# Three matmul passes of split FP32 operands in one PSUM bank instead of two, with another third form of the tokens

## The chip, the cores and the metric

The kernel runs on one NeuronCore of a Trainium2 chip. A core has a matmul engine (TensorE, PE in the profile; its weight loads are PEld), VectorE (DVE), ScalarE (ACT), GpSimd (POOL) and SyncE (SP), which run their own instruction streams and wait for each other on semaphores. Matmuls write to PSUM, which the kernel uses as eight banks of 512 FP32 values in each of 128 partitions. The metric is the device time of one execution in microseconds (us). Lower is better.

## What is computed

Input `x` is (32, 64, 1024) in FP32, with one conditioning row of 128 for each of the 32 samples. Two layers follow one another, each with a residual. The reference, cut to what matters here:

```python
def _L0_ffn_ref(x, A, B, Wr):              # A: (64, 16, 1024), B: (64, 1024, 16)
    scores = xf @ Wr.T                     # 64 experts
    top_vals, top_idx = jax.lax.top_k(scores, 16)
    gates = jax.nn.softmax(top_vals, axis=-1)
    G = zeros.at[rows, top_idx].set(gates)
    h = jnp.einsum('nd,krd->nkr', xf, A)
    out = jnp.einsum('nkr,kdr->nd', h * G[:, :, None], B)
    return out * 2.0

x = x + _L0_ffn_ref(_cond_ref(x, cond_512, ...), A, B, Wr)
x = x + _L1_ffn_ref(_cond_ref(x, cond_512, ...), qweight, scales, zeros, bias)
```

`_cond_ref` is a chain of four modulated convolutions of 3 taps over the 1024 positions (same, upsample, same, downsample), with weights that depend on the sample. `_L1_ffn_ref` is a dense product with a 1024 x 1024 matrix whose entries are unpacked from 4-bit integers.

## The kernel before

**Pairs.** Two samples of 64 channels fill the 128 partitions, so there are 16 pairs in each layer. A pair's convolution result, turned so that the 1024 positions lie on the partitions in 8 blocks of 128, is called its tokens.

**Three phases.** First, for each pair of layer 0: convolutions (`first`, `rest`), then `layer0`, the product with `wa`, which is the router and A side by side (1024 x 1088), then the gates (top 16 of 64, softmax) and their multiplication into the result (`gated`, line 1003, on GpSimd). The result goes to DRAM. Second, for each pair: load it again, transpose it on TensorE (`turned_h`), and in `layer0b` multiply by B (`wb`, 1024 x 1024) and add the residual. Third, for each pair of layer 1: convolutions, and `layer1`, the product with the unpacked matrix. Around 0 to 100 us the layer's factors are made; around 400 to 437 `wb` is prepared; from 590 to 660 the second phase overlaps with the first convolutions of layer 1.

**Split operands.** In this trace a 128x512 matmul on the type fp32r takes TensorE 0.23 us, while one on plain FP32 is two instructions of 0.43 us. So operands are split into an upper part, with its last 12 bits cleared, and the rest, and multiplied as fp32r in several passes. `split` (line 915) makes the upper part of the tokens, `th`, by a shift on VectorE (`high`, line 149) and a copy on ScalarE (line 923), and the lower part, `tl`, on VectorE (line 919). `split_weights` (line 367) does so with the weights, into three forms per block of 128 rows: 0 the upper part (ScalarE, line 375), 1 the lower part (GpSimd, line 374), and 2 the crossed form, upper minus R times lower (VectorE, line 382), with R = 2**12. The first two pairs of layer 0 (`WHOLE`) use plain FP32 instead, while the weights are being split.

**Three passes.** Before the change, `tl` is multiplied by R on ScalarE right after its split (`scaled_low`, line 927). A third form, `td` = `th` - R `tl`, is made by `crossed` on GpSimd (line 935) at the end of the previous pair's turn; it has one buffer. With these, `product` runs passes 0 and 1 (called `Q`: `th` with the upper weights, R `tl` with the lower ones) into one PSUM bank, and pass 2 (called `D`: `td` with the crossed weights) into another. The exact product is (1 + 1/R) times the first bank minus 1/R times the second. `joined` forms it: in `layer0` the first bank by ScalarE (line 976) and then the second by VectorE (line 977); in `layer0b` two VectorE instructions, the second bank into the residual (line 1123) and the first bank plus the residual (line 1124).

**Chunks.** `layer0` cuts the 1088 columns in three (352, 368, 368): Q of chunks 0 and 1, then D of both, then Q and D of chunk 2. Pair 2, the first with split operands, does blocks 0 to 5 of every pass first and then blocks 6 and 7, whose weights are split late. `layer0b` has two chunks of 512: Q, Q, D, D. The last pair goes block by block.

**PSUM.** Three pools share the eight banks: `cps` has three (convolutions, line 832's first reconstruction result, transposes), `mps` one and `fps` four (the products). The second reconstruction result (line 872) lies in `cps`, except in layer 1 from its second pair on, where it lies in `fps`. It is freed by line 919.

**Order.** The order of instructions on each engine is fixed before the run by a planner that goes by the order of the program, by its own estimate of when operands are ready and by free buffers. So program order is followed loosely: matmuls of a convolution stand between those of a product. At run time every engine works strictly in that order.

**Weights of the second phase.** Blocks 0 to 3 of `wb` are split during pair 0 of `layer0b`, blocks 4 to 7 during pair 1; pair 2 is the first to use them.

Of the kernel before, what the change touches and what calls it, by code (L numbers as in the profile page):

```python
# [11 lines left out]
AF = mybir.ActivationFunctionType  # L12
ALU = mybir.AluOpType
# [12 lines left out]
H = 512  # L26
# [6 lines left out]
SCALING = 2.0  # L33
# [7 lines left out]
RADIX = float(1 << BITS)  # L41
# [22 lines left out]
def adaln_ffn_kernel(ctx: ExitStack, tc: tile.TileContext, t, out: bass.AP):  # L64
    nc = tc.nc
# [19 lines left out]
    def fpst(name):  # L85
        return fps.tile([P, H], F32, tag="fps", name=name)
# [67 lines left out]
    done, tbl, outers, uppers = {}, {}, {}, {}  # L154
    WHOLE = (0, 1)
# [624 lines left out]
    def rest(i, n, y, f):  # L780
# [4 lines left out]
        p, h = n // 2, n % 2  # L785
        whole = i == 0 and p in WHOLE
        key = f"x{i}_{p}"
        if h == 0:
            th = tokens("th", f"th{key}", F32 if whole else F32R)
            toks[key] = [th] if whole else [th, tokens("tl", f"tl{key}")]  # L790
        hs = halves[h]
        th = toks[key][0][:, :, hs]
# [7 lines left out]
        if whole:  # L800
            yb, yo = y
            ps = cpst(f"r{i}_{n}")
            for j in range(4):
                for k in range(4):
                    v = (yo, yb)[(j + k) % 2]
                    o = j // 2 + k // 2 + (j % 2) * (k % 2)
# [4 lines left out]
                        start=(k == 0),  # L811
                        stop=(k == 3),
                    )
            c = tbl[i, p][:, h, 1].unsqueeze(1).to_broadcast([P, 2 * 4, C])
# [17 lines left out]
        ps = cpst(f"r{i}_{n}_0")  # L832
        for j in range(2):
# [4 lines left out]
                start=True,  # L838
                stop=True,
            )  # L840
        for j in range(2):
            if nine(i, p):
# [4 lines left out]
                    start=True,  # L847
                    stop=True,
                )
                continue  # L850
            for k in range(2):
# [4 lines left out]
                    start=(k == 0),  # L856
                    stop=(k == 1),
# [11 lines left out]
            m.rearrange("p (q b) -> p q b", q=2).unsqueeze(1).to_broadcast([P, 2, 2, P]),  # L869
            ALU.add,  # L870
        )
        ps = (fpst if i == 1 and p > 0 else cpst)(f"r{i}_{n}_1")
        for j in range(4):
            q, k = j % 2, j // 2
            done["r"] = nc.tensor.matmul(  # L875
# [3 lines left out]
                start=True,  # L879
                stop=True,  # L880
# [6 lines left out]
            re[:, p % 2, h].unsqueeze(1).to_broadcast([P, 2, P]),  # L887
        )
        split(ps, shape, th, toks[key][1][:, :, hs], f"h{i}_{p}_{h}", i == 1 and h == 1 and p > 0)
        if i == 0 and h == 1:  # L890
            scaled_low(toks[key][1])

    def outer(p):

# [27 lines left out]
        else:  # L922
            nc.scalar.copy(hi, h)

    def scaled_low(v):
        v = v.rearrange("p a b -> p (a b)")
        nc.scalar.activation(v, v, AF.Copy, scale=RADIX)  # L927

    toks = {}

    def crossed(key):

        if key in toks and len(toks[key]) == 2:
            td = tokens("td", f"td{key}")
            done["td"] = nc.gpsimd.tensor_tensor(  # L935
                *(v.rearrange("p a b -> p (a b)") for v in (td, *toks[key])), ALU.subtract
            )
            toks[key].append(td)

    def at(k):  # L940
# [3 lines left out]
    def product(chunk, key, ws, order, limbs, ks=range(NC), first=0, last=NC - 1):  # L944


        banks, cols = chunk
        n = len(toks[key])
        for l in limbs:
            if l < n:  # L950
                for k in ks:
                    w = ws[k]
                    if n > 1:
                        w = w[:, l]
                    nc.tensor.matmul(  # L955
                        banks[l == 2],
                        toks[key][l][:, order(k)],
                        w[:, cols],
                        start=(k == first and l != 1),
                        stop=(k == last and l in (2, min(n, 2) - 1)),  # L960
                    )

    Q, D = (0, 1), (2,)
# [1 line left out]
    def layer0(p, ws):  # L965

        hs = wk.tile([P, AW], F32, tag="w4", name=f"hs{p}", bufs=3)
        key = f"x0_{p}"
        whole = p in WHOLE

        def joined(col, w, qd):
            dst = hs[:, col : col + w]
            if whole:
                nc.scalar.copy(dst, qd[0])
                return
            nc.scalar.activation(dst, qd[0], AF.Copy, scale=1.0 + 1.0 / RADIX)
            nc.vector.scalar_tensor_tensor(dst, qd[1], -1.0 / RADIX, dst, ALU.mult, ALU.add)

        ga = tiny.tile([P, E], F32, tag="ga", name=f"ga_{p}")

# [24 lines left out]
        def chunk(c):  # L1005
            a, b = CHUNKS[c]
            w = (b - a) * R + (E if c == 0 else 0)
            col = a * R + (E if c > 0 else 0)
            banks = [fpst(f"h{p}_{c}_{j}")[:, :w] for j in range(1 if whole else 2)]
            return banks, slice(col, col + w)  # L1010

        def done_with(c, ch):
            product(ch, key, ws, at, D)
# [56 lines left out]
    def turned_h(p, hg):  # L1070
        whole = p in WHOLE
        key = f"h{p}"
        th = tokens("th", f"th{key}", F32 if whole else F32R)
        toks[key] = [th] if whole else [th, tokens("tl", f"tl{key}")]
        for g in range(2):
            ps = cpst(f"ht{p}_{g}")
            for c in range(4):
                k = 4 * g + c
                nc.tensor.transpose(  # L1079
                    ps[:, c * P : (c + 1) * P], hg[:, k * P : (k + 1) * P], ident  # L1080
                )
            ks = slice(4 * g, 4 * g + 4)

            def d(v):
                return v[:, ks].rearrange("p a b -> p (a b)")

            if whole:
                nc.scalar.copy(d(th), ps)
            else:
                split(ps, lambda v: v, d(th), d(toks[key][1]), f"hh{p}_{g}")  # L1090
        if not whole:
            scaled_low(toks[key][1])

    residual = {}

# [11 lines left out]

    def layer0b(p, ws):

        whole = p in WHOLE  # L1110
        key = f"h{p}"
        xres = residual.pop(p)
        x1 = wk.tile([P, L], F32, tag="w4", name=f"x1_{p}", bufs=3)
        x4 = x1.rearrange("p (f j) -> p j f", f=4)

        def banks(c):
            return [fpst(f"o{p}_{c}_{j}") for j in range(1 if whole else 2)]

        def joined(c, qd):
            cs = slice(c * H, (c + 1) * H)  # L1120
            v = xres[:, cs]
            if not whole:
                nc.vector.scalar_tensor_tensor(v, qd[1], -SCALING / RADIX, v, ALU.mult, ALU.add)  # L1123
            nc.vector.scalar_tensor_tensor(  # L1124
                x4[:, c * P : (c + 1) * P],
                qd[0].rearrange("p (j f) -> p j f", f=4),
                SCALING if whole else SCALING * (1.0 + 1.0 / RADIX),
                v.rearrange("p (j f) -> p j f", f=4),
                ALU.mult,
                ALU.add,  # L1130
            )

        cols = [slice(c * H, (c + 1) * H) for c in range(2)]
        if p == NP - 1:
            qds = [banks(c) for c in range(2)]

            for part in (Q, D):
                for k in range(4):
                    for ch in zip(qds, cols):
                        product(ch, key, ws, lambda k: k, part, (k,))  # L1140
            yield
            for ch in zip(qds, cols):
                product(ch, key, ws, lambda k: k, Q, range(4, NC))
                yield
            for c, ch in enumerate(zip(qds, cols)):
                product(ch, key, ws, lambda k: k, D, range(4, NC))
                joined(c, qds[c])
                if c == 0:
                    yield
        else:  # L1150
            qds = [banks(c) for c in range(2)]
            for ch in zip(qds, cols):
                product(ch, key, ws, lambda k: k, Q)
            for c, ch in enumerate(zip(qds, cols)):
                product(ch, key, ws, lambda k: k, D)
                joined(c, qds[c])
                yield
        if p not in WHOLE:
            load_residual(p + 1)
# [384 lines left out]
```

## Time and profile before

| | us |
|---|---|
| median of 3 runs | 894.1 |
| the runs | 894.0, 894.1, 895.79 |
| span of the profiled execution, first to last instruction | 893.1 |
| TensorE busy | 866.1 |
| VectorE busy | 723.2 |
| ScalarE busy | 352.4 |
| GpSimd busy | 531.1 |

The profile gives the span of the execution that it shows, not a time of its own; the median of the runs lies 1.0 us above that span. "Busy" is time in which an instruction of the engine runs; matmuls overlap, and their ends are modelled. In a timeline, a line holds the start, the duration, the engine, the line of the kernel, the operation, the output and the input, their shapes and the number of instructions merged; in brackets stand the idle time before them and who ended it. Busy time of the groups of instructions that the change touches, with the mean of one:

| line, engine | what | count | us | mean ns |
|---|---|---|---|---|
| 976, ACT | first bank of a chunk of `layer0` | 42 | 19.9 | 473 |
| 977, DVE | second bank of it | 42 | 22.0 | 525 |
| 1123, DVE | second bank into the residual, `layer0b` | 28 | 18.0 + 1.4 | 692 |
| 1124, DVE | first bank plus residual | 26 + 6 | 28.4 + 6.1 | 1091, 1076 |
| 927, ACT | `tl` times R | 14 + 14 | 14.8 + 14.8 | 1056, 1060 |
| 935, POOL | `td` | 14 + 14 | 34.7 + 34.0 | 2479, 2425 |
| 382, DVE | crossed weights, `wa` and `wb` | 8 + 8 | 11.8 + 15.8 | 1472, 1975 |

### The profile page before, as it was taken

To read this page: it belongs to the slowest core of one execution; us is meant where nothing else is said; L and a number is where in the kernel's file an instruction comes from. 1 tells how busy PE (TensorE), PEld (TensorE's weight loads), DVE (VectorE), ACT (ScalarE), POOL (GpSimd) and SP (SyncE) were. 2 spreads that over 40 slices of the span, in tenths; PEclk is the share of its full clock that TensorE was granted. 3 is DMA by queue.
4 is the path that set the end of the run, shared out by engine and by line. 5 is a ranking of instruction groups with operands and counts; after the bars stand their busy time and mean duration, and the time that the engine had idled before them with its cause. 6 is when DMAs were issued, how large, how long until landed. Compare 5 with 4: busy or idle time off the path is not lost.

```text
span 893.1 us, 14916 instructions
## 1 busy us (share of the span) xinstructions
PE 866.1 (97%) x5033; PEld 775.1 (87%) x5033; DVE 723.2 (81%) x1460; ACT 352.4 (39%) x817; POOL 531.1 (59%) x745
## 2 busy tenths in 40 slices
PE   6989999999999999999999999999999999999997
PEld 4876888999999999994688888888899999999997
DVE  4475898888888888778986765669999999999996
ACT  6444544444444444333332221247333433343340
POOL 7235654666666666556572222343787888888884
PEclk9999999999999999999999999999999999999999
DMA  8632222222232222345475666555543334334321
GB/s 240 155 73 54 54 69 62 88 89 80 79 91 83 81 79 71 106 178 149 139 232 193 201 193 197 189 192 167 164 117 111 98 100 143 114 90 139 122 66 71
DMA packets 49739, 109.81 MB, mean 123 GB/s; under 512 B 13700, under 2 KB 22400, under 8 KB 49664
## 3 DMA queue, kind: packets, MB, share of 16 engines
q1 hardware_dynamic: 48704, 107.88, 39.5%
q10 hardware_dynamic: 960, 0.99, 0.5%
q8 instruction: 40, 0.66, 0.3%
q14 instruction: 35, 0.29, 0.1%
HBM read 70.97 MB, written 37.88 MB: 122 GB/s over the span
## 4 chain that ended last, share of the span: by engine, by line
PE 42%; DVE 7%; POOL 2%; issue 2%; ACT 0%; DVEq 0%; POOLq 0%; ACTq 0%
PE o L955 16%; PE q L1204 11%; PE f L619 3%; PE r L875 3%; PE c L773 2%; PE r L834 1%; PE r L843 1%; PE c L768 1%; PE ht L1079 1%; PE g L596 1%; DVE cv L716 1%; DVE x L1124 1%; PE p L826 1%; DVE rt L866 1%; DVE r L884 0%
## 5 line engine op out<-in xcount | busy, mean ns | idle before, releaser
L716 DVE TENSOR_TENSOR cv<-cv 128x257 f32<-128x257 f32 x120 | 105.8, 913 | 1.3 <-ACT cv L758 0.9
L730 POOL TENSOR_TENSOR cv<-cv 128x256 f32<-128x256 f32 x120 | 77.7, 647 | 29.8 <-DVE cv L716 25.1
L722 POOL TENSOR_TENSOR cv<-cv 128x128 f32<-128x128 f32 x100 | 39.0, 411 | 67.5 <-PE r L843 48.3
L1204 PE MATMUL q<-wq,thx 128*128 128x342 f32 x384 | 73.0, 332 | 2.1 <-ACT thx L913 2.1
L955 PE MATMUL h<-wa,tdx 128*128 128x352 f32 (+1 forms) x336 | 72.2, 351 | 0.2 <-DVE wa L382 0.2
L1204 PE MATMUL q<-wq,tlx 128*128 128x342 f32 x384 | 72.3, 330 | 0.0
L619 PE MATMUL f<-gs,iw 128*128 128x128 f32 (+1 forms) x384 | 68.2, 327 | 0.1
L619 PEld LDWEIGHTS f<-gs,iw 128*128 128x128 f32 x384 | 61.8, 190 | 5.9 <-issue 0.5
L955 PE MATMUL h<-wa,thx 128*128 128x352 f32 (+1 forms) x336 | 64.7, 333 | 0.0
L1204 PEld LDWEIGHTS q<-wq,thx 128*128 128x128 f32 x384 | 60.3, 189 | 4.1 <-ACT thx L913 3.2
L770 ACT ACTIVATE yt<-c,be,al 128x257 f32<-128x257 f32 x56 | 31.7, 567 | 80.4 <-PE c L768 77.3
L875 PE MATMUL r<-cv 128*128 128x128 f32 x480 | 63.4, 274 | 0.0
L1204 PEld LDWEIGHTS q<-wq,tlx 128*128 128x128 f32 x384 | 61.9, 189 | 0.8
L955 PE MATMUL h<-wa,tlx 128*128 128x352 f32 (+1 forms) x336 | 62.4, 327 | 0.0
L955 PE MATMUL o<-wb,thh 128*128 128x512 f32 x224 | 60.4, 402 | 1.5 <-ACT wb L375 1.5
L935 POOL TENSOR_TENSOR tdx<-thx,tlx 128x1024 fp32r<-128x1024 f32 x14 | 34.7, 2479 | 44.5 <-ACT tlx L927 36.2
L955 PEld LDWEIGHTS h<-wa,tdx 128*128 128x128 f32 x336 | 56.9, 188 | 2.4 <-DVE wa L382 0.5
L1123 DVE SCALAR_TENSOR_TENSOR cv<-o,cv 128x512 f32<-128x512 f32 x26 | 18.0, 692 | 50.2 <-PE o L955 50.2
L955 PE MATMUL o<-wb,tlh 128*128 128x512 f32 x224 | 58.4, 397 | 0.0
L875 PEld LDWEIGHTS r<-cv 128*128 128x128 f32 x480 | 58.4, 191 | 0.0
L634 ACT COPY cv<-f 128x256 f32<-128x256 f32 x64 | 24.0, 375 | 83.9 <-PE f L619 46.3
L642 POOL TENSOR_TENSOR cv<-cv 128x256 f32<-128x256 f32 x60 | 50.0, 833 | 11.4 <-ACT cv L637 11.4
(313 smaller groups left out, 2274.6 us busy)
## 6 DMA issues: line engine op xcount, KB each, us to landing
cv<-in_x_dram SPq DMA_DIRECT2D x60, 256.0 KB
cv<-x1e SPq DMA_DIRECT2D x64, 192.5 KB
x1e<-dd SPq DMA_DIRECT2D x16, 514.0 KB
hgd<-hs SPq DMA_DIRECT2D x16, 512.0 KB
hg<-hgd SPq DMA_DIRECT2D x16, 512.0 KB
x1d<-x SPq DMA_DIRECT2D x16, 512.0 KB
xb<-x1d SPq DMA_DIRECT2D x16, 512.0 KB
out_dram<-o SPq DMA_DIRECT2D x15, 512.0 KB
```

The lines of the kernel that those rows point to most:

```text
L619: done["f"] = nc.tensor.matmul(pv[:, n : n + 2 - k], iw[:, e].rearrange("p a b -> p (a b)"), v, start=(m == 0), stop=(m == len(steps) - 1) ...
L634: nc.scalar.copy(f8[:, 0::2], pv[:, :, h])
L642: nc.gpsimd.tensor_tensor(f[:, 4 * P : 6 * P].rearrange("p (a b) -> p a b", b=P), v[:, :, 0], v[:, :, 1], ALU.add,)
L716: nc.vector.tensor_tensor(d[:, k], yo[:, k : k + HQ], yb, ALU.subtract)
L722: nc.gpsimd.tensor_tensor(y[:, YB + k * P : YB + (k + 1) * P], y[:, 2 * k : 2 * k + 2 * P - 1 : 2], y[:, 1 : 2 * P : 2], ALU.subtract,)
L730: nc.gpsimd.tensor_tensor(e[:, :, k], d[:, :, 2 * k : 2 * k + HQ - 2 : 2], d[:, :, 1 : HQ - 1 : 2], ALU.subtract,)
L770: nc.scalar.activation(yt, mid, AF.Identity, bias=be0[:, n : n + 1], scale=a)
L875: done["r"] = nc.tensor.matmul(ps[:, j * P : (j + 1) * P], y[:, YE + (2 * q + k) * P : YE + (2 * q + k + 1) * P], w(q + 2 * k), start=True ...
L935: done["td"] = nc.gpsimd.tensor_tensor(*(v.rearrange("p a b -> p (a b)") for v in (td, *toks[key])), ALU.subtract)
L955: nc.tensor.matmul(banks[l == 2], toks[key][l][:, order(k)], w[:, cols], start=(k == first and l != 1), stop=(k == last and l in (2, min(n ...
L1123: nc.vector.scalar_tensor_tensor(v, qd[1], -SCALING / RADIX, v, ALU.mult, ALU.add)
L1204: nc.tensor.matmul(ps, half[:, k], wq[at(k)][:, c * QC : (c + 1) * QC], start=(k == 0 and j == 0), stop=(k == NC - 1 and j == 1),)
```

## The change

The algebra of the three passes is another. With `th`, `tl` the parts of the tokens and wh, wl those of the weights:

- before: bank one = th wh + (R tl) wl, bank two = (th - R tl)(wh - R wl), product = (1 + 1/R) one - 1/R two
- after: one bank = th wh + tl (wh - R wl) + ((R + 1) tl + th) wl, which is the product itself

So `tl` is no longer scaled, `td` is (R + 1) `tl` + `th`, made by a ScalarE activation into `td` and a GpSimd addition in place, the second pass uses the crossed weights (form 2) and the third the lower ones (form 1). All three passes accumulate in one bank, a chunk takes one bank of `fps`, and the joins shrink: a ScalarE copy in `layer0`, one VectorE instruction in `layer0b`. The second reconstruction result always lies in `fps`. The order of the calls is the same.

```diff
@@ rest
-        ps = (fpst if i == 1 and p > 0 else cpst)(f"r{i}_{n}_1")
+        ps = fpst(f"r{i}_{n}_1")
...
         split(ps, shape, th, toks[key][1][:, :, hs], f"h{i}_{p}_{h}", i == 1 and h == 1 and p > 0)
-        if i == 0 and h == 1:
-            scaled_low(toks[key][1])
@@ crossed
             td = tokens("td", f"td{key}")
-            done["td"] = nc.gpsimd.tensor_tensor(
-                *(v.rearrange("p a b -> p (a b)") for v in (td, *toks[key])), ALU.subtract
-            )
+            v, th, tl = (v.rearrange("p a b -> p (a b)") for v in (td, *toks[key]))
+            nc.scalar.activation(v, tl, AF.Copy, scale=RADIX + 1.0)
+            done["td"] = nc.gpsimd.tensor_tensor(v, v, th, ALU.add)
@@ product
-        banks, cols = chunk
-        n = len(toks[key])
+        bank, cols = chunk
+        n = 3 if len(toks[key]) > 1 else 1
...
-                        w = w[:, l]
+                        w = w[:, (0, 2, 1)[l]]
                     nc.tensor.matmul(
-                        banks[l == 2],
+                        bank,
                         toks[key][l][:, order(k)],
                         w[:, cols],
-                        start=(k == first and l != 1),
-                        stop=(k == last and l in (2, min(n, 2) - 1)),
+                        start=(k == first and l == 0),
+                        stop=(k == last and l == n - 1),
                     )
@@ layer0
-        def joined(col, w, qd):
+        def joined(col, w, bank):
             dst = hs[:, col : col + w]
-            if whole:
-                nc.scalar.copy(dst, qd[0])
-                return
-            nc.scalar.activation(dst, qd[0], AF.Copy, scale=1.0 + 1.0 / RADIX)
-            nc.vector.scalar_tensor_tensor(dst, qd[1], -1.0 / RADIX, dst, ALU.mult, ALU.add)
+            nc.scalar.copy(dst, bank)
...
-            banks = [fpst(f"h{p}_{c}_{j}")[:, :w] for j in range(1 if whole else 2)]
-            return banks, slice(col, col + w)
+            return fpst(f"h{p}_{c}")[:, :w], slice(col, col + w)
@@ turned_h
-        if not whole:
-            scaled_low(toks[key][1])
@@ layer0b
-        def joined(c, qd):
-            cs = slice(c * H, (c + 1) * H)
-            v = xres[:, cs]
-            if not whole:
-                nc.vector.scalar_tensor_tensor(v, qd[1], -SCALING / RADIX, v, ALU.mult, ALU.add)
+        def joined(c, bank):
             nc.vector.scalar_tensor_tensor(
                 x4[:, c * P : (c + 1) * P],
-                qd[0].rearrange("p (j f) -> p j f", f=4),
-                SCALING if whole else SCALING * (1.0 + 1.0 / RADIX),
-                v.rearrange("p (j f) -> p j f", f=4),
+                bank.rearrange("p (j f) -> p j f", f=4),
+                SCALING,
+                xres[:, c * H : (c + 1) * H].rearrange("p (j f) -> p j f", f=4),
                 ALU.mult,
                 ALU.add,
             )
```

## The prediction, made before the changed kernel was run

> **What bounds the kernel now.** I read the page's busy times first, then the busy time of each engine in six stretches, then what TensorE waited for, then the timeline around the places where it waited.
>
> The page, parts 1 and 2:
>
> ```profile
> PE 866.1 (97%) x5033; PEld 775.1 (87%) x5033; DVE 723.2 (81%) x1460; ACT 352.4 (39%) x817; POOL 531.1 (59%) x745
> ...
> PE   6989999999999999999999999999999999999997
> ```
>
> TensorE is idle for 893.1 - 866.1 = 27.0 us in all. The change alters no count and no shape of matmul (three passes before, three after), so this is all it can win. By stretch (columns: span, then PE, PEld, DVE, ACT, POOL busy, granted clock, DMA share, GB/s):
>
> ```profile
> 60.00:160.00 100.00, 96.08 (x538) 82.32 (x538) 71.24 (x163) 43.05 (x95) 53.44 (x63) 1.00 0.25 69
> 160.00:360.00 200.00, 200.00 (x1251) 190.43 (x1251) 173.60 (x409) 92.49 (x212) 120.75 (x165) 1.00 0.26 78
> 360.00:435.00 75.00, 73.46 (x354) 55.86 (x353) 57.63 (x98) 26.65 (x61) 46.76 (x51) 0.99 0.46 147
> 435.00:600.00 165.00, 164.16 (x800) 137.03 (x799) 111.71 (x183) 46.59 (x95) 55.42 (x92) 1.00 0.60 194
> 600.00:720.00 120.00, 116.50 (x743) 108.23 (x742) 115.85 (x232) 50.60 (x123) 87.23 (x138) 1.00 0.44 135
> 720.00:860.00 140.00, 140.00 (x919) 134.96 (x918) 134.14 (x253) 56.82 (x147) 118.55 (x156) 1.00 0.38 116
> ```
>
> From 160 to 360 (layer 0, first products) and from 435 to 600 (second products) TensorE has no gap worth naming. VectorE works 87% and 68% of the time there, beside it, so taking work from it buys nothing. Only 60:160, the change of phase near 430, and 600:720, where VectorE is 97% busy, leave TensorE something to win. The first 60 us (11.4 us idle) and the last 33 (5.8) hold nothing that the change touches. The waits of TensorE (total, times, longest):
>
> ```profile
> PE c L773 <- DVE rt L866: 2.2, 3, 1.1
> PE q L1204 <- ACT thx L913: 2.1, 3, 0.9
> PE r L834 <- POOL cv L648: 1.9, 2, 1.1
> PE c L773 <- DVE tlx L919: 1.8, 2, 1.3
> PE o L955 <- ACT wb L375: 1.5, 2, 0.9
> ```
>
> **Part by part.** *The joins* (edits in `layer0` and `layer0b`). Gone from VectorE: 42 of line 977 at 525 ns (22.0 us) and 28 of line 1123 (18.0 + 1.4 us), 41.4 us in all. On ScalarE the 42 of line 976 (473 ns) become copies; line 974, the same copy of a whole pair, takes 454. They now stand after the third pass. No DMA is added; the stores of lines 1063 and 1160 follow their joins and come up to 0.7 us earlier. The path that sets the end gets nothing from this wherever TensorE is full.
>
> *The third form.* Line 927 (ScalarE, 28 times 1.06 us) goes, an activation of the same size comes, and GpSimd's addition of 2.4 to 2.5 us stays. But the activation writes `td`, which has one buffer, so ScalarE now waits for the last matmul of the pair before, where GpSimd waited. Behind it stand the copies of the composed filters (lines 634 to 637) and `yt` (line 770), which sums and matmuls wait for. In the steady part of layer 0, GpSimd ran so:
>
> ```profile
> 282.29 2.50 POOL L935 TENSOR_TENSOR tdx<-thx,tlx 128x1024 fp32r<-128x1024 f32 x1 [3.59 <-ACT tlx L927]
> ...
> 287.62 0.45 POOL L652 TENSOR_TENSOR cv<-cv 128x128 f32<-128x128 f32 x1
> ```
>
> Line 927 ran at 281.16, the last third-pass matmul ended at 281.19: both conditions are met at the same moment, so nothing moves, except that ScalarE also has the 0.47 us copy of the third chunk there. Line 652 ends at 288.07 and TensorE's line 826, which needs it, starts at 288.20: a margin of 0.13 us. I take 0, since the gating at line 1003 (0.99) can use the time while ScalarE works. The bounds: 0 below (there is no TensorE gap to win) and 0.47 - 0.13 = 0.34 us in each of 13 pairs, 4.4, above. Without line 927, ScalarE's 0.16 us waits before it end too, but the upper half's pass hides them.
>
> *The banks.* The second reconstruction result moves to the pool of four, and a chunk takes one bank, not two. The waits at line 773 for lines 866 and 919 are waits for a bank of the pool of three: 1.12 us at 113.07, 0.57 at 125.00, 1.26 at 620.32.
>
> *The start of the three passes* (pair 2, 103 to 136). The 1.12 us is won, then lost: VectorE is busy without a gap from 109.9, and the crossed weights of block 7 (line 382, 118.11 + 1.29 = 119.40), now needed by the second pass, hold TensorE there. Behind the release stand three matmuls where it was one: +0.3. The 0.57 goes: -0.6. Then GpSimd's `td`, at 127.16 straight after the last matmul of pair 2, comes 1.06 + 0.1 later, and its chain to line 834 (waited for 1.15 us at 135.34) with it: +1.1, less the 0.3 by which that matmul is earlier and 0.3 for three joins less on VectorE. Sum +0.5. Bounds: -0.9 (the 1.15 goes as well, less 0.3 for the release) and +1.2 (the whole move of the chain).
>
> *The crossed weights of the second matrix* (pair 2 of `layer0b`) carry the largest term. TensorE, then VectorE:
>
> ```profile
> 432.28 0.50 PE L955 MATMUL o<-wb,thh 128*128 128x512 f32 x1 [0.91 <-ACT wb L375]
> 432.62 3.37 PE L955 MATMUL o<-wb,tlh 128*128 128x512 f32 x8
> 435.78 2.24 PE L955 MATMUL o<-wb,thh 128*128 128x512 f32 x8
> ```
>
> ```profile
> 433.00 2.31 DVE L382 SCALAR_TENSOR_TENSOR wb<-wb 128x1024 fp32r<-128x1024 f32 x1
> 436.48 1.23 DVE L382 SCALAR_TENSOR_TENSOR wb<-wb 128x1024 fp32r<-128x1024 f32 x1 [1.18 <-POOL wb L374]
> ```
>
> The second pass begins at 432.62 and used the lower weights, which were there. Now it needs the crossed ones, of which block 6 is ready at 435.31 and block 7 at 437.71. Eight matmuls took 3.37, 0.42 each: six end at 435.1, the seventh at 435.7, the eighth starts at 437.7 and ends at 437.95. The other chunk's first pass then starts at 437.95, not 435.78: +2.2. Everything on TensorE stands behind that eighth matmul: its order is fixed before the run. No cover is left, since 435:600 is full. I expect that order unchanged: VectorE ran line 382 of block 7 and even line 212 (437.62) ahead of pair 1's second join (438.49), which shows that the planner thought the weights ready before pair 1's matmuls ended.
>
> A gap also costs clock. Granted clock (column after POOL) behind the two gaps of 0.63 and 0.91 us:
>
> ```profile
> 433.00:434.00 1.00, 1.00 (x4) 0.80 (x3) 1.00 (x2) 0.89 (x4) 1.00 (x1) 0.50 0.94 352
> ...
> 436.00:437.00 1.00, 1.00 (x5) 0.78 (x5) 0.52 (x1) 0.93 (x3) 0.88 (x9) 0.85 0.00 0
> ```
>
> It stood at half for about 3.4 us (432.9 to 436.3), which is 1.7 us of work. A new gap of 2.0 us I price the same: +1.7. About 0.1 comes back, because the other chunk's first pass leaves the old slow stretch. Sum +3.8; bounds 0 (no wait) and 2.2 + 2 x 1.7 = 5.6 (two slow stretches).
>
> The Trainium skill (TensorE: Matmul & The Clock Gate, section Part 1: The HAM clock gate, and the table of section Why this matters for your kernels) speaks otherwise: the clock falls only after an idle window of about 3.4 us, so gaps under some 3 us should be harmless. By that rule the total would be 894.4 in place of 896.1; the rows above show the fall after far shorter gaps, and I go by them.
>
> *The handover to layer 1* (600 to 720; TensorE idle 3.5). The 1.26 at 620.32 goes with the bank. The other 2.2 hang on VectorE, which loses three joins there (597.37, 621.10, 621.95: 2.1 us). Also line 1168, stretched to 2.88 beside GpSimd's `td` at 599.48 where it otherwise takes 0.68, may start before that. I count half of the 2.2, since GpSimd (73% busy) takes part in the same waits: -2.3. Bounds -3.5 and 0.
>
> **Sum.** 0.5 + 3.8 - 2.3 = +2.0. The profiled span is 893.1, the median of the runs 894.1, so 1.0 lies around the span: 895.1 as span, 896.1 as time.
>
> **Rivals.** *The wait does not come* (the other side, not slower): at 432.6 the planner puts the other chunk's matmuls first, or the weights come earlier. It decides once block 7 is ready by 435.6 (432.62 + 7 x 0.42) or nine ready matmuls (2.0 us at 0.227) stand ahead. For it: chunks are already interleaved elsewhere (two of line 773 inside a third pass at 279.5). Against: the order of line 382. Without the 3.8, and with the 0.3 at 119.4 also gone: 894.1 + 0.2 - 2.3 = 892.0. *The wait, but no slow clock*: 896.1 - 1.7 = 894.4; for it, the six matmuls before the gap keep TensorE busier than at 430. *No relief at the handover*: waits only change their name, 898.4; for it, VectorE is still 95% busy there. *GpSimd late in every pair of layer 0*: 896.1 + 4.4 = 900.5; for it, the margin of 0.13; against it, the free time before line 1003. *The change does not do what it says*, when the joins go but their engines were never waited for: true for most of the 41.4 us, and already in the sum.
>
> **Chances.** Forecast 0.40, no wait 0.35, no slow clock 0.09, no relief 0.11, late GpSimd 0.05. A measurement of this kernel tells about 0.2% (1.8 us) from no change. Faster (under 892.3): 0.27 of the no-wait case and 0.01 of the slow-clock one, 0.28. Same: 0.12 + 0.08 + 0.06 + 0.01 = 0.27. Slower (over 895.9): 0.28 + 0.02 + 0.10 + 0.05 = 0.45. Range 891.2 to 899.0: it holds the no-wait case with 0.8 of spare below, and no relief above. The forecast's own range is 894.3 to 897.9.
>
> **What would show it.** Right: a wait of line 955 for line 382 of about 2 us near 433 to 438 and a second half-clock stretch behind it; no wait of line 773 for lines 866 and 919 at 113, 125 and 620; the pair's period of 21.7 us in layer 0 unchanged; TensorE idle in 600:720 near 1.2 us. Wrong: line 955 without that wait, a longer period, or a TensorE order in which the passes stand otherwise.

## The result and the profile after

The changed kernel takes 905.3 us (median of 4 runs, 903.97 to 905.69) where the kernel before took 894.9 beside it (4 runs, 894.0 to 896.62): 1.0116 times the time before, 95% interval 1.0104 to 1.0129. The profiled execution has a span of 903.5 us. The forecast was 896.1, with 899.0 as its upper end. In every run on record the span lies 1.7 to 1.9 us below the time.

The page's busy times and TensorE's row of granted clock, after:

```profile
PE 866.6 (96%) x5033; PEld 777.9 (86%) x5033; DVE 713.0 (79%) x1390; ACT 349.6 (39%) x817; POOL 533.6 (59%) x745
...
PEclk9999999999999999999899999999999999999999
```

TensorE works the same 866 us and idles 10 us longer. VectorE lost 70 instructions that took 41.4 us, yet its busy time fell by 10 only: other instructions of it became longer. In the page's row one slice has a lower clock, the one near 440. Two of the six stretches (columns as in the prediction) hold nearly all of the story:

```profile
435.00:600.00 165.00, 158.60 (x752) 131.52 (x753) 107.71 (x145) 40.17 (x80) 52.91 (x84) 0.97 0.56 186
600.00:720.00 120.00, 115.69 (x719) 106.52 (x718) 109.83 (x219) 51.11 (x124) 82.93 (x130) 1.00 0.43 136
```

The second products, 435 to 600, were full before (0.84 us idle); now 6.4 us are idle there, and the mean clock is 0.97. The handover (600 to 720) was to lose 2.3 us of idle time; it has 0.8 more.

I set the two traces side by side at the same instructions of TensorE (starts in us; the last column is what the difference grew by since the row above):

| instruction of TensorE | before | after | grew by | forecast |
|---|---|---|---|---|
| filters of line 619, before the first pair of three passes | 93.1 | 94.2 | +1.1 | 0 |
| line 619, when three passes run steadily | 150.8 | 151.5 | -0.4 | +0.5 |
| line 619, last pairs of layer 0 | 367.8 | 368.1 | -0.4 | 0 |
| line 232, after pair 2 of `layer0b` | 443.3 | 448.1 | +4.5 | +3.8 |
| line 557, late in the second products | 582.7 | 592.4 | +4.9 | 0 |
| line 619, in layer 1 | 653.9 | 664.3 | +0.7 | -2.3 |
| end of the span | 893.1 | 903.5 | 0.0 | 0 |

The first row is not from the change. A wait of about 2 us of line 596 for line 586 stands near 19 us in most profiles below, and also in the two that are the kernel before with one edit (e4, e11). Where a half-clock stretch follows it, line 619 starts at 94.2 to 94.5 (this profile, e3, e4, e7), and at 92.5 to 93.1 in all others.

**The crossed weights, as forecast.** The timeline of TensorE, after:

```profile
432.57 1.54 PE L949 MATMUL o<-wb,tlh 128*128 128x512 f32 x6
435.30 0.50 PE L949 MATMUL o<-wb,tlh 128*128 128x512 f32 x1 [1.19 <-DVE wb L382]
437.69 0.79 PE L949 MATMUL o<-wb,tlh 128*128 128x512 f32 x1 [1.89 <-DVE wb L382]
438.28 3.62 PE L949 MATMUL o<-wb,thh 128*128 128x512 f32 x8
```

and its busy time in two stretches behind the first gap (columns: span, then PE, PEld, DVE, ACT, POOL busy, granted clock, DMA share, GB/s):

```profile
436.71:440.12 3.41, 2.43 (x6) 1.95 (x7) 3.41 (x5) 0.47 (x3) 0.55 (x9) 0.50 0.00 0
440.12:443.54 3.42, 3.42 (x10) 2.64 (x9) 3.42 (x7) 1.15 (x2) 0.00 (x0) 0.50 0.91 349
```

Blocks 6 and 7 came at 435.30 and 437.69, as read off VectorE's timeline before (435.31, 437.71). What I had not counted: the six matmuls before the gap ran at full clock (1.54 us where eight took 3.37 before), so they finished early and only waited longer. Then eight matmuls took 3.62 us. The clock stood at half (0.50) from 436.71 to 443.54, twice as long as before; the old stretch from 432.9 to 436.3 did not come.

**The second loss, not forecast.** Four engines around line 345, after:

```profile
498.59 1.06 ACT L930 ACTIVATE tdh<-tlh 128x1024 fp32r<-128x1024 f32 x1 [0.40 <-PE o L949]
...
499.83 2.90 POOL L931 TENSOR_TENSOR tdh<-tdh,thh 128x1024 fp32r<-128x1024 f32 x1
500.43 2.85 DVE L1147 TENSOR_TENSOR dd<-x 128x510 f32<-128x510 f32 x1
503.20 0.18 DVE L334 TENSOR_TENSOR cv<-cv 128x32 f32<-128x32 f32 x1
...
503.44 0.23 PE L345 MATMUL rows<-ident,cv 64*32 64x64 f32 x1 [2.06 <-DVE cv L334]
```

The same place before:

```profile
493.95 2.37 POOL L935 TENSOR_TENSOR tdh<-thh,tlh 128x1024 fp32r<-128x1024 f32 x1
...
495.40 0.97 DVE L334 TENSOR_TENSOR cv<-cv 128x32 f32<-128x32 f32 x1
...
496.43 0.23 PE L345 MATMUL rows<-ident,cv 64*32 64x64 f32 x1 [0.53 <-DVE cv L334]
...
497.49 0.68 DVE L1168 TENSOR_TENSOR dd<-x 128x510 f32<-128x510 f32 x1
```

Line 1147 (1168 before) takes 0.68 us; beside GpSimd's addition it took 2.85, and both ended at nearly the same moment (502.73 and 503.28). Before, GpSimd began straight after the last matmul of the pair and fell on another part of VectorE's work. Now ScalarE's step of 1.06 us comes first, and the addition meets the two subtractions of `dd`; behind them stands line 334, and TensorE waits 2.06 us for it. The planner's order on VectorE is another too: before, line 334 stood ahead of these subtractions. At 589.93 the same happens to line 466 (2.36 us where it takes 0.35), and line 557 waits 1.68. The two waits and the half-clock stretch behind the first make the 4.9 us of the table: 2.06 - 0.53, 1.7 (half of 3.4) and 1.68.

**The handover.** The 1.26 us wait for a bank at 620 is gone (line 773 starts at 620.58 without one). In its place: at 613.17 TensorE waits 0.84 for the third form of the last pair, since GpSimd does the copy of line 1154 (0.65) ahead of it, where it came behind it before, and one sum of filters took 1.19 in place of 0.74 (the addition starts at 610.74 against 599.48, with TensorE's matmuls beside it 10.0 later); and the 0.74 us wait for layer 1's token copies became 1.69. Line 596 waits 0.6 us more for ScalarE. VectorE and GpSimd ahead of the wait of 1.69, after:

```profile
647.39 0.70 DVE L883 TENSOR_TENSOR r<-r,rt 128x512 f32<-128x512 f32 x1 [0.47 <-PE f L619]
...
647.68 2.87 POOL L1166 TENSOR_TENSOR o<-xb,aux 128x1024 f32<-128x1024 f32 x1
...
648.13 2.73 DVE L884 COPY_PREDICATED r<-ident,re 128x256 f32<-128x256 int32 x1
...
650.88 0.69 DVE L149 TENSOR_SCALAR h<-r 128x512 int32<-128x512 int32 x1
```

The same two instructions before:

```profile
637.50 2.90 POOL L1187 TENSOR_TENSOR o<-xb,aux 128x1024 f32<-128x1024 f32 x1
...
638.84 1.85 DVE L884 COPY_PREDICATED r<-ident,re 128x256 f32<-128x256 int32 x1
```

Line 884 ended at 650.86, just behind GpSimd's addition of line 1166 (647.68 to 650.55). Before, it began 1.3 us into that addition, took 1.85 and ended in the same way. Counted from the start of TensorE's matmuls of line 619 just before (645.05, before 635.84), VectorE came to line 884 no earlier than before (3.1 us against 3.0), while GpSimd's addition began 1.0 us later (2.6 against 1.7). So VectorE, with the joins gone, won nothing here and waited longer for GpSimd, which had itself waited 0.97 us for VectorE's line 716 at 645.52. Why these came later is not shown.

### The profile page after: what moved, and what is told of

It is laid out like the page before. It is cut to its first block, busy times and chain, and to the rows that moved or that the text cites. A ratio compares the mean times of both kernels' runs of the same rounds, so it can differ in the third digit from the quotient of the medians.

```text
span 903.5 us, 14758 instructions
## 1 busy us (share of the span) xinstructions
PE 866.6 (96%) x5033; PEld 777.9 (86%) x5033; DVE 713.0 (79%) x1390; ACT 349.6 (39%) x817; POOL 533.6 (59%) x745
## 4 chain that ended last, share of the span: by engine, by line
PE 42%; DVE 7%; POOL 2%; issue 2%; ACT 0%; DVEq 0%; POOLq 0%; ACTq 0%
PE o L949 15%; PE q L1183 11%; PE f L619 3%; PE r L875 3%; PE c L773 3%; PE r L834 1%; PE r L843 1%; PE g L596 1%; PE c L768 1%; PE ht L1068 1%; POOL wb L374 1%; DVE nib L434 1%; DVE cv L716 1%; PE p L826 1%; DVE r L884 1%
## 5 line engine op out<-in xcount | busy, mean ns | idle before, releaser
L716 DVE TENSOR_TENSOR cv<-cv 128x257 f32<-128x257 f32 x120 | 108.9, 939 | 1.3 <-ACT cv L758 0.9
L722 POOL TENSOR_TENSOR cv<-cv 128x128 f32<-128x128 f32 x100 | 41.8, 438 | 65.5 <-DVE su L986 53.1
L1103 DVE SCALAR_TENSOR_TENSOR x<-o,cv 128x512 f32<-128x512 f32 x26 | 28.4, 1092 | 56.7 <-PE o L949 56.7
L993 POOL TENSOR_TENSOR hs<-hs,ga 128x368 f32<-128x368 f32 (+1 forms) x48 | 37.6, 798 | 56.7 <-ACT hs L967 50.8
L949 PE MATMUL h<-wa,tdx 128*128 128x352 f32 (+1 forms) x336 | 67.8, 344 | 0.0
L921 ACT CAST thx<-h 128x512 fp32r<-128x512 f32 x45 | 27.9, 619 | 98.8 <-DVE h L149 98.7
L949 PEld LDWEIGHTS h<-wa,tlx 128*128 128x128 f32 x336 | 56.2, 188 | 1.3 <-DVE wa L382 1.3
```

The costliest lines, as they stand in the source:

```text
L716: nc.vector.tensor_tensor(d[:, k], yo[:, k : k + HQ], yb, ALU.subtract)
L722: nc.gpsimd.tensor_tensor(y[:, YB + k * P : YB + (k + 1) * P], y[:, 2 * k : 2 * k + 2 * P - 1 : 2], y[:, 1 : 2 * P : 2], ALU.subtract,)
L949: nc.tensor.matmul(bank, toks[key][l][:, order(k)], w[:, cols], start=(k == first and l == 0), stop=(k == last and l == n - 1),)
L993: nc.gpsimd.tensor_tensor(v, v, g, ALU.mult)
L1103: nc.vector.scalar_tensor_tensor(x4[:, c * P : (c + 1) * P], bank.rearrange("p (j f) -> p j f", f=4), SCALING, xres[:, c * H : (c + 1) * H ...
```

## The experiments

All but e4 and e11 start from the changed kernel; "less" and "above" without a name are against its 905.3. Each was compared with runs of the kernel before on the same chip (median 894.7 for e1 to e4, 894.2 for e5 to e8, 894.7 for e9 to e11); the ratios are to these.

**e1_swap.** In pair 2 of both products the crossed weights come last and the lower ones second, as they did before.

```diff
+    def passes(p):
+        return ((0, 2), (1,)) if p == len(WHOLE) else (Q, D)
...
+        Q, D = passes(p)
```

> The changed kernel, but pair 2 of both products (the first pair with split operands) takes its third pass (third form of the tokens with the lower weights) second, and the pass with the crossed weights last. Theory: in layer0b TensorE stood 1.19 and 1.89 us for the crossed weights of blocks 6 and 7 and then ran at half clock until 443; both go, as does the 1.06 us at 120 in layer 0. TensorE reaches the matmuls of line 232 (448.05 in the changed kernel) near 443.5 to 444, and the time falls by 4 to 5 us, from 905.3 to about 901. Rival: the half-clock stretch belongs to the older 0.9 us wait for the upper weights and stays wherever the passes stand; then 2 to 3 us of gain, 902.5 to 903. Second rival: the planner reorders around the swap and nothing is won, 905.

Measured 900.4 us (1.0060, 1.0039 to 1.0081), 4.9 less than the changed kernel. Both waits for line 382 of `wb` are gone; the waits of lines 345 (2.1) and 557 (1.7) are untouched. In layer 0, 0.7 of the 1.06 us wait for line 382 of `wa` stays. The second pass's weights carry this part.

**e2_scale.** Without the ScalarE step: the lower part is scaled by R early, as before, and the third form is one GpSimd addition. Left out is the product of both lower parts.

```diff
-            nc.scalar.activation(v, tl, AF.Copy, scale=RADIX + 1.0)
-            done["td"] = nc.gpsimd.tensor_tensor(v, v, th, ALU.add)
+            done["td"] = nc.gpsimd.tensor_tensor(v, th, tl, ALU.add)
...
-            ws[:, 2], ws[:, 1], -RADIX, ws[:, 0], ALU.mult, ALU.add
+            ws[:, 2], ws[:, 0], 1.0 / RADIX, ws[:, 1], ALU.mult, ALU.subtract
```

> The changed kernel, but the lower tokens are scaled by R in place right after their split, as before the change; the crossed weights are upper/R minus lower, and the third form is one GpSimd addition of upper and scaled lower tokens. One bank, no joins, same passes; left out is only the product of both lower parts. So the third form no longer has a ScalarE step between the last matmul of the pair before and the GpSimd addition. Theory: that step put GpSimd's 2.4 us addition beside VectorE's subtractions of line 1147 and 466, which it stretched to 2.85 and 2.36, and TensorE stood 2.06 (line 345, with a half-clock stretch behind it) and 1.68 (line 557) for what stands behind those, and 0.84 for the last pair's third form: these three waits fall to 0.5 us or less, VectorE's line 1147 stays at 0.7 near 500, and the time falls by 4.5 to 6 us to about 900. Rival: the waits come from the joins' new place in VectorE's order, not from the ScalarE step: they stay, 905.

Measured 900.7 (1.0071, 1.0050 to 1.0092): 4.6 less. Line 345 waits 1.0, line 557 0.5, the last pair's third form still 0.7; the waits for `wb` stay at 3.1. From line 232 to line 557 TensorE takes 1.1 us longer than in the kernel before, where the changed kernel takes 4.9 longer.

**e3_both.** Both edits.

> Both edits of the two runs before. Theory: the two costs stand in different places and add, so the time falls by 9 to 10 us to about 895 to 896, level with the kernel before the change; the bank at the handover then shows as 1 to 2 us of gain, or not at all. Rival: one of the two hides the other (a pair that comes early waits later), 898 or more.

Measured 898.0 (1.0035, 1.0024 to 1.0046): 7.3 less, where 9.5 would be the sum, and so where the rival put it. It stays 3.4 above the kernel before.

**e4_twostep.** The kernel before, with its third form in two steps: ScalarE writes the negated lower part into `td`, GpSimd adds the upper part. Nothing else of the change.

```diff
-            done["td"] = nc.gpsimd.tensor_tensor(
-                *(v.rearrange("p a b -> p (a b)") for v in (td, *toks[key])), ALU.subtract
-            )
+            v, th, tl = (v.rearrange("p a b -> p (a b)") for v in (td, *toks[key]))
+            nc.scalar.activation(v, tl, AF.Copy, scale=-1.0)
+            done["td"] = nc.gpsimd.tensor_tensor(v, v, th, ALU.add)
```

> The kernel before the change, in which only the third form is made in two steps: ScalarE writes minus the scaled lower tokens into it (an extra 1.06 us activation, after the last matmul that reads the old one), then GpSimd adds the upper tokens in place. Theory: this alone brings the waits of lines 345 and 557 (2 and 1.7 us) and of the last pair's third form, so 4.5 to 6 us, about 899 to 901. Rival: with two banks and the joins in place VectorE's order is another, the addition meets nothing, and the time stays within 1 us of 894.9.

Measured 899.1 (1.0055, 1.0034 to 1.0077), 4.5 above the kernel before, with the new waits in the same places (line 345 1.7, line 557 1.1); the last pair's wait for its third form did not come. VectorE has the order of the kernel before here, and line 334 itself is stretched:

```profile
499.71 2.15 DVE L334 TENSOR_TENSOR cv<-cv 128x32 f32<-128x32 f32 x1
```

It ends at 501.86, with GpSimd's addition (499.45 to 501.81). So the wait does not need VectorE's new order, and that order alone does not bring it (e7 and e9 below have it, without the wait). The step is a cause, not a companion: between lines 232 and 557 it costs the kernel before 3.8 us, as much as its removal gave there in e2. The whole 4.5 is less sure: its profile is of the longest of the four runs (902.63), 7.7 us behind the one before, and 3.0 of these arise in layer 0, 1.7 by a half-clock stretch at 116.8, and 1.4 by the half-clock stretch near 21 us described above. Also, line 927 stays in e4, so ScalarE has 28 activations more than in either kernel (379.8 us busy).

**e5_bank.** One line back: the second reconstruction result in the pool of three banks again.

```diff
-        ps = fpst(f"r{i}_{n}_1")
+        ps = (fpst if i == 1 and p > 0 else cpst)(f"r{i}_{n}_1")
```

> The changed kernel with one line back as it was before: the second reconstruction result of layer 0 and of layer 1's first pair lies again in the pool of three banks (all else as changed). Theory A (the bank waits that went were given back as other waits on the same engines, net 0.6 us): 904.5 to 906.5 us; the convolution's waits for a bank (line 773) come back at the start of the three passes and at the handover, about 1.3 us each, and the wait of layer 1's first product for its token copies falls from 3.0 to about 2 us. Rival B (the move of the bank itself spoils the order at the handover and costs some 2 us): 902.5 to 903.5, and TensorE idle in 600:720 falls from 4.3 to near 3. Rival C (the move is worth the 2.3 us of the prediction, hidden by other losses): 907 or more, TensorE idle in 600:720 at 6 or more.

Measured 918.1 (1.0262, 1.0248 to 1.0276): 12.8 more than the changed kernel. Theories A and B fell. C's two conditions hold (TensorE idles 6.8 us in 600:720), but its size was too small, and most of the cost lies in layer 0. Its waits of TensorE begin with

```profile
PE c L773 <- DVE tlx L917: 8.6, 11, 0.9
```

and a pair of layer 0 shows one of them:

```profile
284.61 0.69 PE L949 MATMUL h<-wa,tdx 128*128 128x368 f32 x2
286.12 0.67 PE L773 MATMUL c<-cv,c 128*128 128x256 f32 x2 [0.82 <-DVE tlx L917]
```

Nearly every pair waits 0.8 us for the bank that VectorE's subtraction frees, and the filter matmuls of line 619 start 22.7 us apart where they stood 21.7 apart in both kernels: 9.9 us over layer 0, and 3.2 more at the handover. The kernel before does not wait there: its matmul of line 773 at 279.48 starts 0.96 us before line 919 at 280.44, so it stood on another bank. The moved bank is thus no bonus of the change but part of what makes it bearable, and the profile of before could not show its worth at the three waits that I added up.

**e6_both_bank.** e3_both with the same line back.

> The kernel of e3_both (tokens' lower part scaled early, one-step addition without the product of both lower parts, crossed weights last in pair 2) with the second reconstruction result back in the pool of three. e3_both lies 3.4 us above the kernel before, and TensorE idles 2 us more than before at the handover. Theory A: 897.5 to 899 us, as e3_both. Rival B (the bank's move costs at the handover): 895.5 to 896.5, TensorE idle in 600:720 from 5.5 to near 3.5. Rival C: 900 or more.

Measured 908.1 (1.0167, 1.0148 to 1.0185), 10.1 above e3_both, with 12 of those waits (9.0 us), as rival C had it. The bank is not what keeps e3_both above the kernel before.

**e7_vector.** The third form by one VectorE instruction; nothing is left out.

```diff
-            nc.scalar.activation(v, tl, AF.Copy, scale=RADIX + 1.0)
-            done["td"] = nc.gpsimd.tensor_tensor(v, v, th, ALU.add)
+            done["td"] = nc.vector.scalar_tensor_tensor(
+                v, tl, RADIX + 1.0, th, ALU.mult, ALU.add
+            )
```

> The changed kernel with the third form made by one VectorE instruction ((R+1) times lower plus upper) in place of the ScalarE step and the GpSimd addition. The theory says that the waits of lines 345 (2.1), 557 (1.7) and for tdh at the last pair (0.9), with the half-clock stretch behind 345, come from the ScalarE step pushing GpSimd's addition beside VectorE's small instructions: they fall below 0.5 each and 4.5 to 6 us go, 899.5 to 901 us; the waits for the crossed weights in pair 2 (3.1) stay. Rival (they come from VectorE's load or the order, whoever adds): they stay or move, 904 or more. A second risk: VectorE has 1.1 us a pair more in layer 0 and would be late for the pair's matmuls: 904 or more with new waits in 160:360 where 0.5 us idle stood.

Measured 896.3 (1.0026, 1.0015 to 1.0037): 9.0 less, better than expected. The waits for lines 334 and 466 and for `tdh` are gone. The busy times show what VectorE gained:

```profile
PE 864.2 (97%) x5033; PEld 777.0 (87%) x5033; DVE 692.8 (77%) x1418; ACT 322.1 (36%) x789; POOL 478.4 (53%) x717
```

VectorE has 28 instructions more, of 37.8 us (14 of 1.36 and 14 of 1.34), and is busy 20.2 us less than in the changed kernel. The rest of its work, the same instructions as there, is thus 58.0 us shorter without GpSimd's 28 additions beside it. The waits for `wb` stay (3.4 us).

**e8_vector_swap.** e7 with the passes of e1.

> As e7_vector, and in pair 2 of both products the crossed weights stand in the last pass and the lower weights in the second (e1_swap). Theory: the two costs are apart, 895 to 897 us, and the waits for the crossed weights go from 3.1 to below 0.5; nothing of the computation is left out, so this would be the change without its two losses. If a rest like e3_both's 3.4 us stays: 897 to 899. Rival (as in e7_vector): 900 or more.

Measured 890.0 (0.9953, 0.9940 to 0.9965), faster than both kernels and than every case that was expected, and 6.3 below e7; TensorE waits no longer for any block of `wb`.

**e9_vector_second and e10_vector_first** split e7: the VectorE instruction for the second products alone, and for layer 0 alone.

```diff
+            if key[0] == "h":
...
+            if key[0] == "x":
```

> The changed kernel with the third form of the second products alone (layer0b) made by one VectorE instruction; that of layer 0 stays with ScalarE and GpSimd. e7_vector, with both on VectorE, lay 9.0 us below the changed kernel. Theory: the waits of lines 345 (2.1) and 557 (1.7), the one for tdh at the last pair (0.8) and one half-clock stretch (1.7) belong to this part: 6 us go, 898.5 to 900.5 us, those waits below 0.5 each. Rival (it is layer 0's addition that sets the planner's order everywhere): 903 or more, the waits stay.

> The other half of e7_vector: the third form of layer 0's products alone is made by one VectorE instruction. Theory: GpSimd's addition of 2.5 us stands ahead of its work for the convolution at pair 3, so the wait of line 834 for GpSimd's line 648 (1.9) falls to about 0.8, and the pair's period of 21.66 us stays: 2.5 to 3.5 us go, 901.5 to 903.5; the waits of lines 345, 557 and for tdh stay as in the changed kernel. Rival (VectorE, with 1.1 us more in each pair, is late): 905 or more and a longer period.

Measured 898.6 (1.0044, 1.0026 to 1.0061) and 901.7 (1.0074, 1.0062 to 1.0087): 6.7 and 3.6 less than the changed kernel, 10.3 together where e7 gave 9.0. In e9 the waits for lines 334 and 466 and for `tdh` go and line 834 still waits 2.6 for GpSimd's line 648; in e10 that falls to 1.3 and the others stay (2.1, 1.7, 0.8). Each loss has its own place, as expected. In e9 VectorE runs at the place of line 345 so:

```profile
497.59 1.21 DVE L931 SCALAR_TENSOR_TENSOR tdh<-tlh,thh 128x1024 fp32r<-128x1024 f32 x1
```

with the subtractions of `dd` behind it at 0.68 each again, and line 345 without a wait for VectorE.

**e11_before_vector.** The kernel before, two banks and joins as they were, with its third form subtracted by VectorE.

```diff
-            done["td"] = nc.gpsimd.tensor_tensor(
+            done["td"] = nc.vector.tensor_tensor(
```

> The kernel before with its third form (upper minus scaled lower) made by a VectorE subtraction in place of GpSimd's; the joins of two banks stay. e8_vector_swap lies 4.2 us below the kernel before; this tells how much of that is GpSimd's addition alone. Theory: the addition on GpSimd cost the kernel before its 1.1 us wait of line 834 at pair 3 and some time near 430: 891 to 892.5, that is, 1 to 2.5 us of e8's gain are then due to the one bank itself. Rival (with 22 us of joins in layer 0 and 20 in the second products still on it, VectorE is late when it also makes the third form): 896 or more, with waits of TensorE for VectorE in 160:360.

Measured 889.7 (0.9942, 0.9928 to 0.9956), more than was expected and level with e8 (888.35 to 891.12 against 888.69 to 891.96). So the 4 to 5 us by which e8 beats the kernel before come with the move of GpSimd's addition, which cost the kernel before as well; the single bank, with its two losses repaired, gives nothing that can be measured. Not all of it need be VectorE held up by GpSimd. Of the 5.6 us between the two profiles, 2.7 arise between layer 0's last pairs and line 232, where TensorE waits 0.6 us instead of 1.5 for the upper weights and the half-clock stretch is missing, and 2.3 by the last pairs of layer 0. How much of this is GpSimd's own other work, done sooner, was not separated. Busy times:

```profile
PE 861.2 (97%) x5033; PEld 773.1 (87%) x5033; DVE 724.1 (82%) x1488; ACT 352.4 (40%) x817; POOL 472.7 (53%) x717
```

VectorE took 28 subtractions on (18.6 + 17.6 us) and is busy 0.9 us more than before: the rest of its work is thus 35 us shorter without GpSimd's additions beside it. The joins' 41.4 us are still on it, and TensorE is nevertheless full from 160 to 360 (200.00 of 200 us).

## Why the prediction was right and wrong

The change costs 10.4 us where 2.0 were forecast. The miss of 9.2 us against 896.1 is, by the table, +4.9 in the second products, +3.0 at the handover, +1.1 near 20 us, +0.7 at the crossed weights and -1.3 in layer 0; the last 0.8 is not of the kernels, since 1.0 stood for the 1.8 us that lie between span and time.

**Right.** That the change makes the kernel slower, though most of what it costs was not foreseen, and the largest term with its mechanism: pair 2 of `layer0b` waits for the crossed weights and pays a half-clock stretch. The table has +4.5 for +3.8, and e1 takes 4.9 back with the first product's pair 2. As forecast, one half-clock stretch more came, two for one, so the upper bound's case of two more did not. But they were not the old one and a new one: the old one went, and a double one came behind the new gaps. From 428 to line 232 TensorE idles 4.1 us where it idled 1.5, so +2.6 for the +2.2 of the wait; it works 5.9 us at half clock where it worked 3.4, by which I estimate +1.2 for +1.7. The remaining 0.7 has no place in either. The order was not changed by the planner, so the rival without a wait fell; and the rival without a slow clock fell too. Right also that the joins buy nothing where TensorE is full: layer 0 keeps its period of 21.7, and e8 against e11 shows it for the whole kernel. That the start of the three passes hardly moves (+0.5) measured -0.4, in part by luck: TensorE's wait for line 866 was to go and is still 0.73 us at 114.21, and line 834 waits 1.86 for GpSimd, not 1.15.

**Wrong: "the third form", at 0.** This is the step that failed. I worked it out for layer 0 alone, where it held (-0.4 over 217 us), bounded it by layer 0's pairs alone, and let the second products off as full. But GpSimd's addition was priced there as work of GpSimd: who waits for it. In the second products its price is what it does to VectorE beside it, and moving it by ScalarE's 1.06 us changed what stood beside it. (In layer 0 it is GpSimd's own work that is waited for: e10 takes 3.6 back, with line 834's wait from 2.6 to 1.3.) The stretch was in the rows I had read (line 1168 at 2.88 us beside `td` for 0.68, which I used at the handover as a possible gain), and the moved addition should have been followed through the second products as well, with VectorE's work beside it. The table has +4.9 up to line 557 for it; e4 puts 3.8 there on the step alone, e2 without the step takes 3.8 back there, and e9 takes 6.7 back in all.

**Wrong: the handover, -2.3.** It gave +0.7. The bank's wait went as forecast, but waits of 0.84 and 1.69 came. The first comes from what GpSimd does ahead of the addition at the last pair, not from ScalarE's step: e2, without the step and with the copy behind the addition, keeps 0.7 of it with the longer sum (1.20); e4, with the step and the order of before, does not have it, nor do e7 and e9. In the second, VectorE was no earlier at line 884 and was held until GpSimd's line 1166 ended, which had begun 1.0 us later. "VectorE is 97% busy" was read as work to be taken off; part of it was waiting for GpSimd, which taking work off does not shorten. The rival of no relief had the outcome, that waits only change their name, at 0.11, but not the reason.

**Wrong in its scope: the bank.** Counted at three waits, its move is worth 12.8 us to the changed kernel (e5), in places that the kernel before does not show.

The 1.1 us of the first row are put down to no part of the change. What holds e3_both 3.4 above the kernel before is settled in part. In its profile (of the longest of its runs, 4.5 us behind), 2.0 us arise between lines 232 and 557, where line 345 still waits 1.0, and 1.6 at the handover; the rest lies in half-clock stretches near 21 and 137 us, less 1.5 won before line 232. At the handover TensorE idles 5.5 us in place of 3.5, and GpSimd's addition still stands there in one step; e8, without it, still idles 4.2 us there. How much of that is the order and how much the stretched line 884 was not tried.

## What to carry to other kernels

Price a GpSimd instruction by what it holds up on VectorE, too, and at every place where it is moved: a step of 1 us ahead of it cost some 4 us here, by waits that mostly name VectorE, not GpSimd. An instruction of 2.4 us on GpSimd was cheaper as 1.3 us on the busier VectorE. Where passes are interchanged, ask at the first pair which operand of each is ready last, and put that one last.

## What the runs showed of the hardware

**The clock goes by windows.** But for the one that the end of the span cuts off, the half-clock stretches of all runs are 3.4 us or twice that, and their starts lie on one grid: 20.3, 436.7 and 505.0 us in the changed kernel are 122 and 20 times 3.41 apart. These windows go by the idle time within one of them, not by the length of one gap: two gaps of 0.63 and 0.91 us brought half clock before, one of 1.68 did not after. Two windows of the changed kernel, each with the next one (columns as above):

```profile
501.57:504.98 3.41, 1.54 (x7) 1.26 (x8) 3.41 (x5) 1.17 (x3) 1.16 (x1) 1.00 0.98 339
504.98:508.40 3.42, 3.42 (x10) 2.65 (x9) 0.80 (x2) 0.26 (x1) 0.10 (x1) 0.50 0.83 270
590.31:593.72 3.41, 1.73 (x9) 1.11 (x9) 3.41 (x4) 0.45 (x2) 1.92 (x1) 1.00 0.93 297
593.72:597.13 3.41, 3.41 (x17) 2.81 (x15) 1.57 (x3) 1.18 (x3) 0.00 (x0) 1.00 0.68 242
```

With 1.87 us of idle time the next window ran at half, with 1.68 at full clock. Over the runs it fell after windows at full clock with 1.54 to 2.86 us of idle time and held after some with up to 1.83; matmul ends are modelled, so the border is not sharper than that. A wait of some 2 us may thus cost 1.7 us more (half of 3.4) or nothing, by where the grid happens to lie in that execution: near 19 us line 596 waits 1.95 us in e3 and runs at half clock behind it, and waits 2.19 in e6, split over two windows, and does not. The four runs of e1 spread in the same sense, from 898.31 us at a mean clock of 1.000 to 902.21 at 0.993. The Trainium skill (TensorE: Matmul & The Clock Gate, Part 1: The HAM clock gate) has the window, 3413 ns and free-running, and that agrees. The advice in its section Why this matters for your kernels, to avoid gaps above some 3 us, does not reach far enough here, since gaps of 1.19 and 1.89 us, and one of 2.06, brought half clock.

**Some instructions of VectorE wait for GpSimd.** Instructions of VectorE that take 0.35 and 0.68 us took 2.36 and 2.85 beside a GpSimd addition of 2.85 and 2.90 and ended within 0.6 us of it. The Trainium skill (SBUF — State Buffer, section SBUF: two separate sides) states that a VectorE instruction with two inputs in SBUF and a GpSimd instruction that reads SBUF hold a shared pair of ports in turn, each for its whole length. The rows agree: instructions that read two inputs from SBUF are held, and the instruction after the subtractions runs at its usual 0.18, while line 1124 before, which reads one of its two inputs from PSUM, took its usual 1.09 us at 494.46, beside GpSimd's addition (493.95 to 496.32).
